# The last batch's shared result in an attention and mixture-of-experts kernel: four parts behind the last expert, each with its own addition to the output

## The chip, the cores and the metric

The kernel runs on one core of a Trainium2 chip. The metric is the device time of one execution in microseconds (us). Before the change three timed runs gave 1715.2, 1713.54 and 1716.4, a median of 1715.2. The profile is of one further execution.

## The reference

Input x has 4 batches of 512 tokens with 512 features; a context of 4 x 1601 rows goes with it. The layer is a cross attention (16 heads; an image part and a text part of the context with a softmax each) added to x, and then a mixture of experts added to the result:

```python
x = x + _L0_xattn_ref(_layernorm(x), ctx_2048, ...)
x = x + _L0_ffn_ref(_layernorm(x), ...)
```

The second part matters here. A router picks 4 of 32 experts for each of the 2048 tokens, each expert takes at most 80 tokens, and a shared expert runs over all tokens:

```python
G = jnp.einsum('ecd,edi->eci', Xp, W_gate)
U = jnp.einsum('ecd,edi->eci', Xp, W_up)
Y = jnp.einsum('eci,eid->ecd', jax.nn.silu(G) * U, W_down)
Yf = Y.reshape(EC, d) * slots_w[:, None]
out = jnp.zeros((T, d), x.dtype).at[slots_token].add(Yf)
shared = jax.nn.silu(x @ shared_gate.T) * (x @ shared_up.T) @ shared_down.T
return (out + shared).reshape(b, s, d)
```

Everything is in float32. The output is 2048 rows of 512 numbers, 2 KB a row.

## The kernel before

The attention of the four batches comes first and takes most of the time. The program writes the order of work of every engine out by hand: small functions are called one after another, and each engine (TensorE for matmuls, ScalarE, VectorE, GpSimd and SyncE, which issues most DMAs) runs its instructions in that order, waiting for others by semaphores.

The mixture of experts takes some 380 us at the end. First come the shared expert's parts for the first three batches (`units`), with the routing of the tokens between them. `shared` (L923) makes for each batch four `gate` parts (L945), four `up` parts (L954) and four `down` parts (L965), each one a product of four matmuls into one PSUM bank. `gate` applies Silu on ScalarE into a tile hT, `up` multiplies by the second product on VectorE. For batches 0 to 2 (`n < BEFORE`) `down` adds the stored attention result and writes 128 rows of the output with a plain DMA from SyncE's queue (L976). For batch 3 the attention result is already in the output (L457), and `down` copies its product by ScalarE into a tile `ys` (L980). The fourth `down` of that batch issues one DMA on GpSimd's queue that adds all 512 rows, 1 MB, to the output in memory (L983). In that tile a partition holds four consecutive rows of the output, 8 KB; to bring this about, `gate` and `up` of batch 3 read their PSUM bank in steps of four tokens (`by_token` and `as_tiles`, L934 and L937).

`shared` returns two lists. The first, `units`, runs in a loop at L1071. The second, `between`, holds the twelve parts of batch 3, and runs inside the loop over the experts at L1099. One turn of that loop does, for expert e: `gate_up(e)` (16 matmuls over 80 tokens), the issue of the gate and up weights for expert e + 5, on SyncE's queue (five buffers for each weight), `gather(e + 7)`, an indirect DMA on GpSimd's queue that fetches the tokens of a later expert, `turn(e + 2)`, which transposes gathered tokens, `down(e - 1)`, and then as many parts of `between` as are due by a count.

`down(e)` of an expert (L1029) scales its product on ScalarE into a tile `y` (four buffers) and issues an indirect DMA on GpSimd's queue that adds its 80 rows to the output (L1037). Each such addition may touch any row of the output, so each waits until the one before it has landed, whichever kind that was. The additions thus form a line on GpSimd's queue, with the gathers between them: additions of experts 0 to 25, the addition of `ys`, additions of experts 26 to 31.

The parts that are due are counted by

```python
while done < n_between and done * (E - 4) < n_between * e:
    between.pop(0)()
    done += 1
```

With 12 parts in `between` they come behind the experts' down parts at e = 1, 3, 5, 8, 10, 12, 15, 17, 19, 22, 24 and 26. PSUM's eight banks are handed out in turn (`psum`, L125), and the large tiles `wide` (L138) and the row tiles `rowt` (L147, five buffers) as well.

Of the kernel before, what the change touches and what calls it, by code (L numbers as in the profile page):

```python
# [12 lines left out]
AF = mybir.ActivationFunctionType  # L13
ALU = mybir.AluOpType
# [4 lines left out]
P = 128  # L19
B, L, D = 4, 512, 512  # L20
# [6 lines left out]
NQ = L // P  # L27
# [31 lines left out]
@with_exitstack  # L59
def xattn_moe_kernel(ctx: ExitStack, tc: tile.TileContext, a: dict, out: bass.AP):  # L60
    nc = tc.nc

    dram = ctx.enter_context(tc.tile_pool(name="dram", bufs=1, space=DRAM))
    x1_d = dram.tile([T, D], F32, name="x1_d")

    xw_d = dram.tile([T, D + E], F32, name="xw_d")
    xnT_d = dram.tile([P, NC, T], F32, name="xnT_d")
    den_d = dram.tile([B * NC, 2 * NG4, L], F32, name="den_d")
    rec_d = dram.tile([B * NC, 2 * NG4, L], F32, name="rec_d")

    const = ctx.enter_context(tc.tile_pool(name="const", bufs=1))
    ident = const.tile([P, P], F32, name="ident")
    make_identity(nc, ident)
    mhalf = const.tile([P, 8], F32, name="mhalf")
    nc.gpsimd.memset(mhalf, -0.5)
    logits = const.tile([P, NT, E], F32, name="logits")

    with tc.manual_schedule():
        body(tc, a, ident, mhalf, logits, x1_d, xw_d, xnT_d, den_d, rec_d, out)


BEFORE = 3
# [27 lines left out]
def body(ctx, tc, a, ident, mhalf, logits, x1_d, xw_d, xnT_d, den_d, rec_d, out):  # L110

    nc = tc.nc
# [12 lines left out]
    def psum(dt=F32):  # L125

        shape = [P, 512] if dt is F32 else [P, NQ, P]
        banks.append(banks.pop(0))
        return ring.tile(shape, dt, name="ps", tag=f"bank{banks[-1]}")
# [8 lines left out]
    def wide(name, keep=False):  # L138

        n = wides.pop(0)  # L140
        t = pt.tile([P, NC, 512], F32, name=name, tag=f"wide{n}")
        if keep:
            return t, n
        wides.append(n)
        return t
# [4 lines left out]
    def held(name):  # L150
        return hold.tile([P, D], F32, name=name, tag="hold")
# [9 lines left out]
    def weight(name, tile_=None, tag=None):  # L161
        t = w.tile([P, NC, D], F32, name=name, tag=tag or name) if tile_ is None else tile_
        nc.sync.dma_start(t, a[name])
        return t
# [14 lines left out]
    _, n, s0, _ = BLOCKS[0]  # L179
# [42 lines left out]
    def project(ps, lhsT, rhs):  # L222

        for c in range(NC):
            nc.tensor.matmul(ps, lhsT=lhsT(c), rhs=rhs(c), start=c == 0, stop=c == NC - 1)
# [447 lines left out]
    for n in range(2):  # L673
        t = w.tile([P, NQ, P], BF16, name=f"parts{n}", tag=f"parts{n}")
# [6 lines left out]
    for b in range(B):  # L681
# [88 lines left out]
        for bl in range(NB):  # L770
            for c in range(NC):
# [7 lines left out]
                n = 7 if bl < 2 else 0  # L779
# [143 lines left out]
    def shared():  # L923


        units = [[], []]
        downs = []
        xTs = {0: first_xT[0]}

        def fetch_x(n):  # L930
            xTs[n] = wide("xT")
            nc.sync.dma_start(xTs[n], xnT_d[:, :, n * L:(n + 1) * L])

        def by_token(hT, ic):  # L934
            return hT[:, ic, :].rearrange("p (j q) -> p j q", q=P)

        def as_tiles(ps, n):  # L937


            return ps.rearrange("p (j q) -> p j q", q=P) if n < BEFORE else ps.rearrange("p (q j) -> p j q", j=NQ)  # L940

        for n in range(B):
            t = {}

            def gate(ic, n=n, t=t):  # L945
                if ic == 0:
                    t["hT"] = wide("hT")
                if ic == 2 and n + 1 < B:
                    fetch_x(n + 1)
                ps = psum()  # L950
                project(ps, lambda k: sg[:, k, ic * P:(ic + 1) * P], lambda k: xTs[n][:, k, :])
                nc.scalar.activation(by_token(t["hT"], ic), as_tiles(ps, n), AF.Silu)

            def up(ic, n=n, t=t):  # L954
                ps = psum()
                project(ps, lambda k: su[:, k, ic * P:(ic + 1) * P], lambda k: xTs[n][:, k, :])
                nc.vector.tensor_tensor(by_token(t["hT"], ic), by_token(t["hT"], ic), as_tiles(ps, n), ALU.mult)
                if n == 0 and ic == NC - 1:
                    wides.append(first_xT[1])

            def fetch(j, n=n, t=t):
                t[j] = held("x1r")
                nc.sync.dma_start(t[j], x1_d[n * L + j * P:n * L + (j + 1) * P, :])

            def down(j, n=n, t=t, fetch=fetch):  # L965
                rows = slice(n * L + j * P, n * L + (j + 1) * P)
                if n < BEFORE:
                    if j == 0:
                        fetch(0)
                    if j + 1 < NQ:  # L970
                        fetch(j + 1)
                ps = psum()
                project(ps, lambda k: t["hT"][:, k, j * P:(j + 1) * P], lambda k: sd[:, k, :])
                if n < BEFORE:
                    nc.vector.tensor_tensor(t[j], t[j], ps, ALU.add)
                    nc.sync.dma_start(out[rows, :], t[j])  # L976
                    return
                if j == 0:
                    t["ys"] = wide("ys")
                nc.scalar.copy(t["ys"][:, j, :], ps)  # L980
                if j == NQ - 1:
                    to = out[n * L:(n + 1) * L, :].rearrange("(p j) d -> p j d", j=NQ)
                    nc.gpsimd.dma_start(to, t["ys"], accum_op=ALU.add)  # L983

            to = units[n >= BEFORE]
            if n == BEFORE:
                units[0] += downs
                downs = []
            for ic in range(NC):
                to += [partial(gate, ic), partial(up, ic)]  # L990
                if ic < 2:
                    to += downs[2 * ic:2 * ic + 2]
            downs = [partial(down, j) for j in range(NQ)]
        units[1] += downs
        return units

    def expert_parts():
# [48 lines left out]

        return weights, gather, turn, gate_up, down

    units, between = shared()
    wo = weight("o_w", wide("wo"))  # L1050
    for u in units[:2]:
        u()
# [46 lines left out]
    for e in range(E + 1):  # L1099
# [12 lines left out]
        while done < n_between and done * (E - 4) < n_between * e:  # L1112
            between.pop(0)()
            done += 1

# [1 line left out]


# [33 lines left out]
```

## Time and profile before

| what | us |
|---|---|
| median of three timed runs | 1715.2 |
| time of the profiled execution | 1718.64 |
| its span | 1716.8 |
| TensorE busy in it | 1681.6 (98%) |
| GpSimd busy | 864.1 (50%) |
| VectorE busy | 981.4 (57%) |
| ScalarE busy | 650.6 (38%) |
| first addition of an expert's result issued at | 1491.44 |
| addition of the last batch's shared result issued at | 1675.39 |
| last addition of an expert's result issued at | 1709.25 |

Times inside the profile count from the start of the span. A line in order of time gives start, duration, engine, source line, operation, the names written and read, the count, and in brackets how long the engine had been idle and what ended that. PE is TensorE, PEld its weight load, ACT is ScalarE, DVE VectorE, POOL GpSimd, SP SyncE. A busy TensorE is one that has matmuls in its pipeline, not one at its peak. In a table of stretches each row gives the window, then the busy time of the five engines with their numbers of instructions, the clock granted to TensorE, the mean share of time that the 16 DMA engines were busy, and GB/s. A line of a DMA queue gives packets, MB and the time that these packets took as a share of the 16 engines' window.

### The profile page before, as it was taken

The page shows a single profiled execution, that of the slowest core. Times are in us where ns is not written, and L with a number is a line of the kernel's source. Part 1 is how long each engine was busy: PE and PEld are TensorE (multiplying, and loading weights), DVE is VectorE, ACT ScalarE, POOL GpSimd, SP SyncE. Part 2 cuts the span into 40 slices and gives each one's busy share as a digit, 9 for nine tenths or more (in the row PEclk, how much of TensorE's full clock was granted, in tenths as well). Part 3 has the DMA queues.
Part 4 walks back from the last instruction along what each step waited for, and adds up shares of the span by engine and source line. Part 5 has one row for each costly group of instructions (what it writes and reads, how often), then busy time and mean ns, then how long its engine had stood idle before and what let it go on. Part 6 is the DMA issues. An engine that isn't in the chain of part 4 may idle for free. (4 is left out here: it accounts for less than half of the span.)

```text
span 1716.8 us, 29451 instructions
## 1 busy us (share of the span) xinstructions
PE 1681.6 (98%) x11753; PEld 881.2 (51%) x11753; DVE 981.4 (57%) x2016; ACT 650.6 (38%) x1378; POOL 864.1 (50%) x615
## 2 busy tenths in 40 slices
PE   8999999999999999999999999999999999999995
PEld 4554444456544444565444445644443454677774
DVE  3765554857555557976665579676657667111100
ACT  2135456611454565114555651145547210011111
POOL 3246977333669853337688533286793110233322
PEclk9999999999999999999999999999999999999998
DMA  7000000312000004020000040300002463599883
GB/s 232 1 1 1 27 27 2 114 64 70 30 2 26 26 3 163 19 77 20 5 24 27 15 152 21 105 14 15 2 14 89 145 230 132 176 271 278 264 258 61
DMA packets 67961, 137.35 MB, mean 80 GB/s; under 512 B 16112, under 2 KB 28528, under 8 KB 65648
## 3 DMA queue, kind: packets, MB, share of 16 engines
q1 hardware_dynamic: 61552, 122.01, 21.2%
q0 software_dynamic: 5264, 11.87, 3.6%
q8 instruction: 93, 1.52, 0.4%
q10 hardware_dynamic: 1008, 1.59, 0.3%
q14 instruction: 44, 0.36, 0.1%
HBM read 112.63 MB, written 22.81 MB: 79 GB/s over the span
## 5 line engine op out<-in xcount | busy, mean ns | idle before, releaser
L372 ACT ACTIVATE pT<-ps 128x512 f32<-128x512 f32 (+1 forms) x832 | 429.5, 604 | 342.5 <-PE ps L371 332.0
L334 DVE TENSOR_REDUCE mx<-ps 128x1 f32<-128x512 f32 (+1 forms) x576 | 330.9, 616 | 265.0 <-PE ps L320 265.0
L387 POOL TENSOR_TENSOR acc<-acc,pT 128x1024 f32<-128x1024 f32 x192 | 445.6, 2359 | 3.0 <-ACT pT L372 2.6
L379 PE MATMUL po<-pT,v 128*32 128x512 f32 (+2 forms) x1792 | 222.0, 603 | 0.0
L290 PEld LDWEIGHTS ps<-v_w,cT 128*128 128x128 f32 (+1 forms) x1408 | 168.9, 186 | 102.2 <-DVE mx L334 56.1
L371 PE MATMUL ps<-qT,kT 32*128 32x512 f32 (+1 forms) x1664 | 213.8, 587 | 0.0
L320 PE MATMUL ps<-kT,qT 32*128 32x512 f32 (+1 forms) x1536 | 206.1, 549 | 0.0
L290 PE MATMUL ps<-v_w,cT 128*128 128x128 f32 (+1 forms) x1408 | 197.7, 284 | 0.0
L231 PE MATMUL ps<-cT,wk 128*128 128x512 f32 (+1 forms) x384 | 156.9, 554 | 6.0 <-DMA wk<-in_k_w 6.0
L308 DVE TENSOR_REDUCE mx<-ps 128x1 f32<-128x512 f32 (+2 forms) x256 | 128.1, 562 | 5.2 <-PE ps L305 5.2
L1037 POOL DMA_INDIRECT out<-y,tok x32 | 45.5, 1422 | 149.2 <-DMA out<-y,tok 84.0
L231 PEld LDWEIGHTS ps<-cT,wk 128*128 128x128 f32 x384 | 70.6, 193 | 76.4 <-issue 55.3
L1027 DVE TENSOR_TENSOR ehT<-ehT,ps 128x160 f32<-128x160 f32 x32 | 10.3, 321 | 172.9 <-ACT ehT L1026 134.4
L368 PEld LDWEIGHTS <-pick 32*128 32x128 bf16 (+1 forms) x832 | 21.6, 91 | 165.7 <-issue 164.0
L298 ACT COPY v<-ps 128x128 f32<-128x128 f32 (+1 forms) x208 | 60.1, 289 | 117.7 <-PE ps L290 117.3
L238 POOL TENSOR_TENSOR sq_k<-sq_k,sq 128x512 f32<-128x512 f32 (+2 forms) x48 | 49.6, 1033 | 103.7 <-ACT sq L235 103.4
L394 POOL TENSOR_TENSOR acc<-pT 128x1024 f32<-128x1024 f32 x24 | 56.1, 2360 | 86.9 <-ACT pT L372 54.3
L387 POOL TENSOR_TENSOR pT<-pT 65x1024 f32<-65x1024 f32 x24 | 56.0, 2350 | 86.8 <-PE po L379 78.0
L387 DVE TENSOR_TENSOR acc<-acc,pT 128x1024 f32<-128x1024 f32 (+1 forms) x72 | 97.7, 1404 | 2.1 <-ACT pT L372 2.1
L320 PEld LDWEIGHTS ps<-kT,qT 32*128 32x128 f32 x1536 | 82.0, 183 | 30.8 <-issue 10.1
L379 PEld LDWEIGHTS po<-pT,v 128*32 128x32 f32 (+2 forms) x1792 | 34.7, 107 | 118.6 <-issue 109.3
L368 PE MATMUL ps<-mT,pick 32*128 32x512 bf16 (+1 forms) x832 | 82.5, 385 | 2.4 <-ACT mT L359 2.4
(209 smaller groups left out, 2188.8 us busy)
## 6 DMA issues: line engine op xcount, KB each, us to landing
W_gate<-in_W_gate SPq DMA_DIRECT2D x32, 512.0 KB
W_up<-in_W_up SPq DMA_DIRECT2D x32, 512.0 KB
W_down<-in_W_down SPq DMA_DIRECT2D x32, 512.0 KB
rb<-rec_d SPq DMA_DIRECT2D x64, 128.0 KB
xt<-in_x SPq DMA_DIRECT2D x30, 256.0 KB
cT<-in_ctxT SPq DMA_DIRECT2D x7, 1024.0 KB
wki<-in_k_img_w SPq DMA_DIRECT2D x4, 1024.0 KB
wo<-in_o_w SPq DMA_DIRECT2D x4, 1024.0 KB
```

The lines of the kernel that those rows point to most:

```text
L231: nc.tensor.matmul(ps[:, :n], lhsT=wt[:, k, c * P:(c + 1) * P], rhs=xT[:, k, to], start=k == 0, stop=k == NC - 1)
L290: nc.tensor.matmul(ps[lo:hi, :], lhsT=cTs[bl][:, k, at:at + hi - lo], rhs=ws[bl == NB - 1][:, k, c * P:(c + 1) * P], start=k == 0, stop=k ...
L298: nc.scalar.copy(v[:n, t, :], ps[:n])
L308: nc.vector.tensor_reduce(mx[:, qt, g, bl:bl + 1], ps[:, :n], AX.X, ALU.max, negate=True)
L320: nc.tensor.matmul(ps[:, j * n:(j + 1) * n], lhsT=qT[r:r + HD, c, q * P:(q + 1) * P], rhs=kT[r:r + HD, c, k0:k0 + n], start=True, stop=True,)
L334: nc.vector.tensor_reduce(mx[:, qt, g, i:i + 1], ps[:, :m], AX.X, ALU.max, negate=True)
L368: nc.tensor.matmul(ps[:n], lhsT=pick[r:r + HD, kind(t), :n], rhs=mT[r:r + HD, :], start=True, stop=False)
L371: nc.tensor.matmul(ps[:n], lhsT=kT[r:r + HD, c, t * P:t * P + n], rhs=qT[r:r + HD, c, :], start=False, stop=True)
L372: nc.scalar.activation(pT[:n, g, :], ps[:n], AF.Exp)
L379: nc.tensor.matmul(po[r:r + HD, :], lhsT=v[rows, t, r:r + HD], rhs=pT[rows, g, :], start=start, stop=stop)
L387: (nc.vector if idle else nc.gpsimd).tensor_tensor(to[rows, h, :], to[rows, h, :], pT[rows, h, :], ALU.add)
L394: (nc.vector if idle else nc.gpsimd).tensor_tensor(acc[:, h, :], pTs[0][:, h, :], pTs[1][:, h, :], ALU.add)
```

## The change

The four `down` parts of batch 3 leave the list that runs inside the expert loop. They form a third list, `ends`, which runs after the loop, behind the last expert. Each of them copies its product into a row tile of its own and issues an addition of its own, on GpSimd's queue, to its 128 rows of the output (256 KB, 2 KB a row). `gate` and `up` read PSUM and write hT in plain order for every batch. With 8 parts left in `between`, the count puts them behind e = 1, 4, 8, 11, 15, 18, 22 and 25. Of the four new additions the first waits for the last expert's addition and for its copy, the others for their copies alone.

```diff
-        units = [[], []]
+        units = [[], [], []]
...
-                nc.scalar.activation(by_token(t["hT"], ic), as_tiles(ps, n), AF.Silu)
+                nc.scalar.activation(t["hT"][:, ic, :], ps, AF.Silu)
...
-                nc.vector.tensor_tensor(by_token(t["hT"], ic), by_token(t["hT"], ic), as_tiles(ps, n), ALU.mult)
+                nc.vector.tensor_tensor(t["hT"][:, ic, :], t["hT"][:, ic, :], ps, ALU.mult)
...
-                if j == 0:
-                    t["ys"] = wide("ys")
-                nc.scalar.copy(t["ys"][:, j, :], ps)
-                if j == NQ - 1:
-                    to = out[n * L:(n + 1) * L, :].rearrange("(p j) d -> p j d", j=NQ)
-                    nc.gpsimd.dma_start(to, t["ys"], accum_op=ALU.add)
+                y = rowt("ys")
+                nc.scalar.copy(y, ps)
+                nc.gpsimd.dma_start(out[rows, :], y, accum_op=ALU.add)
...
-            to = units[n >= BEFORE]
-            if n == BEFORE:
+            to = units[n == B - 1]
+            if n == B - 1:
...
             downs = [partial(down, j) for j in range(NQ)]
-        units[1] += downs
+            if n >= BEFORE:
+                units[2] += downs
+                downs = []
...
-    units, between = shared()
+    units, between, ends = shared()
...
+    for f in ends:
+        f()
```

More of the change, by code (lines that the diff above doesn't have):

```diff
@@ L932, in fetch_x @@
             nc.sync.dma_start(xTs[n], xnT_d[:, :, n * L:(n + 1) * L])
[L934 to L940, printed above, removed]
         for n in range(B):
```

## Prediction

> **What bounds the kernel now.** I read the page first, then the chain of waits, then the last 240 us by stretches and in order of time. The profiled execution has a span of 1716.8 us and a time of 1718.64; the three timed runs have a median of 1715.2. I make the sum on the span and carry the difference over to 1715.2. What a measurement of this kernel can tell from no change is about 0.2%, 3.4 us.
>
> The chain that ended last, and the stretches around the experts:
>
> ```profile
> DMA out<-y,tok 1%; POOLq L1148 0%; POOLq L1037 0%
> ```
>
> ```profile
> core 0: us, PE busy (x) PEld busy (x) DVE busy (x) ACT busy (x) POOL busy (x), PEclk, DMA share, GB/s
> 1500.00:1660.00 160.00, 160.00 (x994) 116.56 (x993) 19.34 (x50) 25.66 (x52) 53.02 (x45) 1.00 0.90 272
> 1661.00:1671.20 10.20, 10.20 (x61) 7.21 (x61) 0.72 (x2) 2.23 (x4) 1.89 (x2) 1.00 0.86 276
> 1671.20:1675.40 4.20, 4.20 (x30) 3.12 (x30) 0.72 (x2) 0.30 (x1) 0.93 (x2) 1.00 0.35 43
> 1690.47:1709.25 18.78, 8.19 (x43) 4.92 (x41) 0.52 (x2) 2.35 (x4) 5.64 (x4) 0.80 0.28 35
> ```
>
> The chain sees only the end: expert results added to the output (L1037), each held by the one before. The stretches show why TensorE is not the end. It is occupied until some 1698, while the DMA engines, 0.90 busy with weights until 1671, drop to 0.28 in the last 19 us, where nothing but those additions is left. The same additions in order of time, on GpSimd's queue:
>
> ```profile
> 1627.43 1.42 POOL L1037 DMA_INDIRECT out<-y,tok  x1 [5.09 <-ACT y L1036]
> 1629.16 0.93 POOL L1002 DMA_INDIRECT xp<-xw_d,tok  x1 [0.30 <-issue]
> 1635.64 1.42 POOL L1037 DMA_INDIRECT out<-y,tok  x1 [5.56 <-DMA out<-y,tok]
> 1642.92 1.42 POOL L1037 DMA_INDIRECT out<-y,tok  x1 [4.63 <-DMA out<-y,tok]
> ...
> 1670.73 1.39 POOL L1037 DMA_INDIRECT out<-y,tok  x1 [5.51 <-ACT ys L980]
> 1675.39 0.95 POOL L983 DMA_DIRECT2D out<-ys  x1 [3.27 <-issue]
> 1685.80 1.47 POOL L1037 DMA_INDIRECT out<-y,tok  x1 [9.45 <-DMA out<-ys]
> 1690.47 1.42 POOL L1037 DMA_INDIRECT out<-y,tok  x1 [3.20 <-ACT ehT L1026]
> ...
> 1709.25 1.41 POOL L1037 DMA_INDIRECT out<-y,tok  x1 [3.32 <-DMA out<-y,tok]
> ```
>
> The column to read is the start. Quiet, one addition follows another after 1690.47 - 1685.80 = 4.67; from 1685.80 to 1709.25 there are five such steps, 4.69 each. With weights in flight it is 8.21 (1627.43 to 1635.64) or 7.28. Additions 1 (issued at 1500.40) to 25 (1670.73) take 170.33 us, 7.10 a step. The single addition of the last batch's shared result, 1 MB, holds the queue from 1675.39 to 1685.80: 10.41. So the line of additions ends the kernel, and from addition 2 (1507.20) on its 1716.8 is: 23 steps (163.53) + 4.66 + 10.41 + five quiet steps (23.45) + 7.55 from the last issue to the end.
>
> TensorE sets when each y exists:
>
> ```profile
> 1666.26 3.60 PE L225 MATMUL ps<-shared_down,hT 128*128 128x512 f32 x8
> ...
> 1669.69 1.91 PE L225 MATMUL ps<-xpT,W_gate 128*128 128x80 f32 x16
> ...
> 1675.22 1.91 PE L225 MATMUL ps<-xpT,W_gate 128*128 128x80 f32 x16
> ...
> 1680.75 1.91 PE L225 MATMUL ps<-xpT,W_gate 128*128 128x80 f32 x16
> ```
>
> An expert costs it 1680.75 - 1675.22 = 5.53, a shared part 1669.69 - 1666.26 = 3.43.
>
> **The change, part by part.** *Down parts to the end.* Four parts of 3.43 leave the expert loop and follow the last expert; TensorE's sum is unchanged and still ends near 1698.7, with the last copy to ys (0.59 on ScalarE) by 1699.9. In place of twelve parts the loop holds eight, behind experts 1, 4, 8, 11, 15, 18, 22, 25 instead of 1, 3, 5, 8, 10, 12, 15, 17, 19, 22, 24, 26. The first part stands where it stood, so nothing moves before addition 2 at 1507.20. Behind it TensorE runs at 5.53 + 8 x 3.43 / 25 = 6.6 an expert instead of 7.10, and asks for weights that much faster.
>
> *The addition to the end.* The 10.41 between additions 25 and 26 goes; the queue runs on from 25 to 26 in an ordinary step. It comes back behind addition 31: the first of the four waits for addition 31 to land and for its ys; the other three wait only for ScalarE's copies, so they are issued together, as nine gathers in the trace were, 1.21 us apart. The bytes are the same 1 MB, in rows of 2 KB instead of 8. Bounds: the four quiet steps from 1690.47 to 1709.25 keep the engines busy 0.28 x 18.78 / 4 = 1.31 us for the 164 KB of one, 3.38 of a step being waits around it; 1 MB in such rows is 8.4 us, and 11.8 with the waits. From below, the old addition itself in the window 1676.30 to 1685.80:
>
> ```profile
> q0 software_dynamic: 144, 1.05, 59.8%
> ```
>
> 59.8% of 9.50 us is 5.7 for 1.05 MB on GpSimd's queue, 9.1 with the waits; the rest went to a weight load beside it. I take the row of the same bytes, 10.41, between them. From its landing to the end there are 7.55 - 4.69 = 2.86 as now. So this move alone costs nothing: 10.41 leaves the middle and 10.41 returns.
>
> *What is left: the steps.* Between 1507.20 and the end the new kernel has 29 steps up to addition 31, then 4.69 for its landing, 10.41 and 2.86. It equals the old one when the 29 steps take 1716.8 - 1507.2 - 17.96 = 191.64 us. Steps under weights cost p each, quiet ones 4.69. The weights of the last expert's gate and up are gone at 1671.2 (share 0.86, then 0.35); three fewer parts stand ahead of them, 10.3 us, so quiet could begin at 1661. With L = length under weights (153.8 to 1661) the 29 steps take L + (29 - L/p) x 4.69; they equal 191.64 at p = 7.34.
>
> *The price p.* Of the 24 steps from addition 1 to 25, eighteen ended with the landing of the addition before; they average 7.17 (6.62 to 8.21). The other six ended only when y came: there the line had caught up with TensorE. In the new kernel TensorE runs ahead and the line never catches up, so every step is of the first kind. And weights are denser: 0.90 x 7.10 / 6.6 = 0.97 of the DMA engines. The excess over quiet, 2.48, grows as this does, to 2.67, p = 7.36. Then the stretches without a shared part: two or three experts long now, three or four afterwards. The steps that begin behind the first expert of today's stretches of three are 7.54, 7.00, 7.07, 7.95, 8.21 and 7.28, mean 7.51, or 7.73 with the excess scaled alike. With 14 experts in the first two places of a stretch at 7.36 and 10 in later places at 7.73, p = 7.51. Stretches of four lie beyond what the trace shows, and its longest step is 8.21; I take 7.6. At 0.97 the weights themselves come late by some 2 us, so quiet begins at 1663, L = 155.8.
>
> Sum: 155.8 + (29 - 20.5) x 4.69 = 195.7, against 191.64: **+4.0**. Span 1720.8, time 1715.2 + 4.0 = 1719.2.
>
> *Costed at nothing.* Silu and product of the last batch write hT straight (ScalarE 0.60 in all 16 runs of L952 and VectorE 0.66 to 0.69 in those of L957, old order and plain alike). The four copies to ys lie on ScalarE while the line is at additions 26 to 31; uncovered they would cost 0.59 each. y has four buffers: with the line some 20 us behind, ScalarE's y 27 waits a few us for addition 23, and what is queued behind it is the next expert's Silu; TensorE has 20 us of idle tail before that touches the end. SP issues the same loads in the same order; gathers stay ahead by seven experts.
>
> The Trainium skill ("DMA: Bandwidth & Descriptors", Anatomy of one DMA) puts a fixed cost of about 2.0 us and bytes / 436e3 on each transfer issued by GpSimd, and asks for 1 MiB at a time. By it one transfer is 4.4 and four in line 10.4, an estimate of +6.0 for this change. This trace has the single one at 10.41, beside weights, so above the page's figure.
>
> **The rivals.** *The line gains (faster).* Place: the steps from 1507 to 1661. In the stretches with the engines full (share 0.98 to 1.01) the steps are 7.00, 7.18, 6.68 and 6.69, mean 6.89: a full queue need not mean long steps. Then 153.8 + (29 - 22.3) x 4.69 = 185.2, -6.4, time 1708.8. It decides from p below 7.34. Against it: these windows contain a shared part each. TensorE sets the floor: a last ys at 1699.9 and a quiet addition, 4.69 + 2.86 + 0.8 for its extra rows, end at 1708.3, -8.5.
>
> *It evens out.* p stays at 7.17 and quiet begins at 1661: 189.2, -2.4, time 1712.8. For it: the interference is that of a fixed number of weight bytes. Against it: six cheap steps are lost.
>
> *The four additions go in line.* If each is held until the one before has landed, each costs 4.69 + 0.8 = 5.5, 22.0 for 10.41: +11.6 on top of -2.4, time 1724.4. For it: one queue, one tensor. Against it: their rows are disjoint and no wait is written. (The page's fixed cost would work this way.)
>
> **How the numbers follow.** Forecast (p above 7.5) 0.40, gains 0.23, evens out 0.30, in line 0.07. Faster by over 0.2%: 0.23. Within: 0.30. Slower: 0.47. The range runs from 1708, just beyond the gaining line, to 1726: p = 8.0 with quiet at 1663 is 155.8 + (29 - 19.5) x 4.69 = 200.4, +8.7, and 1.4 more for a tail at its upper bound, 1725.3; the additions in line lie inside. The forecast's own range, 1717 to 1726, starts where the tail is at its lower bound and p at 7.55.
>
> **What would show it.** Right: addition 23 issued near 1663, steps under weights near 7.6, quiet steps 4.7, addition 31 near 1703, four issues of ys 1.2 apart near 1707, TensorE idle from 1699. Wrong: steps under weights of 7.3 or less, additions again released by ScalarE, ys waiting for ys, or TensorE stopped by late weights before 1661, which would lengthen everything.

## The result and the profile after

| | before | changed |
|---|---|---|
| median of 20 timed runs, us | 1716.6 | 1709.35 |
| lowest and highest | 1712.83, 1720.87 | 1708.25, 1717.04 |
| span of the profiled execution | 1716.8 | 1706.7 |

The ratio is 0.9968, with a 95% interval of 0.9958 to 0.9978: faster by 0.3%, where +0.2% was forecast. Measured again later (experiment 8), the changed kernel gave 0.9975 (0.9965 to 0.9986). Of the 20 runs of the changed kernel in the table, thirteen lie at 1708 to 1710 and seven at 1713 to 1717; the profile is of one of the thirteen, and no trace shows what the seven do differently. The spans differ by 10.1 us and the medians by 7.3, because the profile before is of an execution 2.0 us above its median (1718.64) and the one after 1.0 below (1708.38). What follows is read from the profiles.

The page of the changed kernel still ends with the line of additions:

```profile
DMA out<-y,tok 1%; POOL out L972 0%; POOLq L1140 0%; POOLq L1028 0%; POOLq L972 0%
```

The line itself, on GpSimd's queue in order of time (start, duration, engine, line, operation, in brackets the idle time before):

```profile
1506.95 1.41 POOL L1028 DMA_INDIRECT out<-y,tok  x1 [4.73 <-issue]
...
1583.84 1.42 POOL L1028 DMA_INDIRECT out<-y,tok  x1 [4.79 <-DMA out<-y,tok]
...
1588.44 1.42 POOL L1028 DMA_INDIRECT out<-y,tok  x1 [1.95 <-ACT ehT L1017]
...
1621.50 1.42 POOL L1028 DMA_INDIRECT out<-y,tok  x1 [4.82 <-DMA out<-y,tok]
...
1629.66 1.42 POOL L1028 DMA_INDIRECT out<-y,tok  x1 [5.51 <-DMA out<-y,tok]
...
1650.58 1.42 POOL L1028 DMA_INDIRECT out<-y,tok  x1 [5.85 <-DMA out<-y,tok]
...
1662.05 1.39 POOL L1028 DMA_INDIRECT out<-y,tok  x1 [3.58 <-ACT y L1027]
...
1690.09 1.39 POOL L1028 DMA_INDIRECT out<-y,tok  x1 [3.15 <-DMA out<-y,tok]
1694.53 2.74 POOL L972 DMA_DIRECT2D out<-ys  x3 [3.05 <-DMA out<-y,tok]
1698.75 0.86 POOL L972 DMA_DIRECT2D out<-ys  x1 [1.48 <-ACT ys L971]
```

Addition 2 is issued at 1506.95 (1507.20 before), addition 23 at 1650.58 (1657.18), addition 25 at 1662.05 (1670.73), addition 31 at 1690.09 (1709.25). So 8.7 us are gained by addition 25: 6.4 in the 21 steps from addition 2 to 23 (143.63 us instead of 149.98) and 2.1 in the two steps behind them, where the weights end sooner. Between additions 25 and 31, where the 1 MB stood, 10.5 more are gained, and the end gives 9.1 back: 16.61 us follow addition 31 instead of 7.55. Steps under weights spread widely: 8.16 from 1621.50, but 4.60 from 1583.84, as cheap as a quiet one, in the midst of the weights. From addition 2 on every y is ready 2 to 10 us before its addition; an engine named in the brackets there had long been done.

Its stretches (window, busy time of the engines, clock, share of the DMA engines, GB/s):

```profile
1500.00:1660.00 160.00, 160.00 (x1042) 120.06 (x1042) 20.79 (x54) 25.81 (x52) 54.00 (x46) 1.00 0.92 288
1660.00:1670.00 10.00, 10.00 (x79) 8.49 (x78) 0.72 (x2) 1.79 (x4) 2.78 (x2) 1.00 0.44 93
1670.00:1680.00 10.00, 10.00 (x70) 7.84 (x69) 1.04 (x3) 1.86 (x4) 2.78 (x2) 1.00 0.28 35
```

288 GB/s instead of 272, and the DMA engines are quiet from the 1660s. TensorE (1042 matmuls in the first window instead of 994) never stops for weights there.

### The profile page after: what moved, and what is told of

The parts are those of the page before. It is cut to its first block, busy times and chain, and to the rows that moved or that the text cites. A ratio compares the mean times of both kernels' runs of the same rounds, so it can differ in the third digit from the quotient of the medians.

```text
span 1706.7 us, 29452 instructions
## 1 busy us (share of the span) xinstructions
PE 1681.3 (99%) x11753; PEld 881.2 (52%) x11753; DVE 981.0 (57%) x2016; ACT 651.1 (38%) x1378; POOL 866.9 (51%) x618
## 5 line engine op out<-in xcount | busy, mean ns | idle before, releaser
L1018 DVE TENSOR_TENSOR ehT<-ehT,ps 128x160 f32<-128x160 f32 x32 | 10.3, 321 | 158.5 <-ACT ehT L1017 158.5
L394 POOL TENSOR_TENSOR acc<-pT 128x1024 f32<-128x1024 f32 x24 | 56.1, 2360 | 86.9 <-ACT pT L372 54.3
L320 PEld LDWEIGHTS ps<-kT,qT 32*128 32x128 f32 x1536 | 82.0, 183 | 30.8 <-issue 10.1
## 6 DMA issues: line engine op xcount, KB each, us to landing
wki<-in_k_img_w SPq DMA_DIRECT2D x4, 1024.0 KB, 10.5
```

The lines of the kernel that those rows point to most:

```text
L320: nc.tensor.matmul(ps[:, j * n:(j + 1) * n], lhsT=qT[r:r + HD, c, q * P:(q + 1) * P], rhs=kT[r:r + HD, c, k0:k0 + n], start=True, stop=True,)
L394: (nc.vector if idle else nc.gpsimd).tensor_tensor(acc[:, h, :], pTs[0][:, h, :], pTs[1][:, h, :], ALU.add)
```

## The experiments

The theories are A: the line was held up by y, and TensorE running ahead is what helped. B: the 1 MB addition in the middle of the line was what cost. D: dense weights set the length of the steps, as the prediction had it. C, F, G and H are stated where they are tested. Ratios are to the kernel before, with 95% intervals.

### 1. The additions moved alone

```diff
-                nc.gpsimd.dma_start(out[rows, :], y, accum_op=ALU.add)
+                units[2].append(lambda: nc.gpsimd.dma_start(out[rows, :], y, accum_op=ALU.add))
...
-                units[2] += downs
+                units[1] += downs
```

> The four down parts stay inside the expert loop at their old places (TensorE 7.10 us an expert); only the four additions go behind the last expert's. Theory A (the line of additions lost some 11 us waiting for y, and TensorE running ahead is what removed that): the steps up to addition 25 stay as before, addition 25 near 1670.7, the y of experts 26 to 31 come every 5.53, so addition 31 near 1702.7 and the span near 1719, a ratio of 1.000 to 1.002. Theory B (the 1 MB addition in the middle of the line was what cost): the span falls to 1706 to 1709 as in the changed kernel, a ratio near 0.996.

Ratio 1.0016 (1.0007 to 1.0025), span 1719.4. The end of its line:

```profile
1676.88 1.39 POOL L1028 DMA_INDIRECT out<-y,tok  x1 [6.48 <-ACT y L1027]
1682.41 1.39 POOL L1028 DMA_INDIRECT out<-y,tok  x1 [4.14 <-ACT y L1027]
...
1707.15 3.62 POOL L972 DMA_DIRECT2D out<-ys  x4 [2.71 <-DMA out<-y,tok]
```

Freed of the 1 MB, the line waits for y, 5.53 us an expert from 1676.88 on, and the four additions then come on top. B falls: moving the additions without the parts loses 0.2%.

### 2. The parts last, with one addition

```diff
-        units[1] += downs
+        units[2] += downs
...
+    for f in ends:
+        f()
```

> The four down parts go behind the last expert, but their result is added in one addition of 1 MB with rows of 8 KB, as before the change. Theory A: steps up to addition 31 as in the changed kernel (1690 for addition 31); the one addition waits for the last copy (1698.5) instead of starting at 1694.5, so the span is 4 to 6 us above the changed kernel's, near 1712, a ratio of 0.997. Theory C (the small rows and four issues cost more than they save): the span is at or below the changed kernel's 1706.7, a ratio of 0.995 or less.

Ratio 0.9971 (0.9959 to 0.9983), span 1709.8. Addition 31 is issued at 1690.17, as in the changed kernel, and the one addition when the last copy is done:

```profile
1698.54 0.96 POOL L983 DMA_DIRECT2D out<-ys  x1 [6.98 <-ACT ys L980]
```

It ends 11.3 us later; the changed kernel has three of its four under way by then, for a span 3.1 us shorter in the profiles (4 to 6 expected). The intervals of the two ratios overlap, so what this part of the change is worth isn't clear of the noise. C, that small rows cost more than they save, asked for a span of 1706.7 or less and a ratio of 0.995 or less, and falls by both.

### 3. TensorE ahead, the addition in the middle

Left out are the four down products; hT is copied to ys, and the 1 MB is added behind expert 25.

```diff
-                ps = psum()
-                project(ps, lambda k: t["hT"][:, k, j * P:(j + 1) * P], lambda k: sd[:, k, :])
...
-                nc.scalar.copy(t["ys"][:, j, :], ps)
+                nc.scalar.copy(t["ys"][:, j, :], t["hT"][:, j, :])
...
-        units[1] += downs
+        units[2] += downs
...
+        if e == 26:
+            for f in ends:
+                f()
```

> Left out: the down products of the last batch (hT is copied to ys instead). gate and up stand at the changed kernel's places, so TensorE runs ahead as there, but the 1 MB addition stays behind expert 25. Theory A: the steps to addition 25 are as in the changed kernel (near 1662), then 5 + 10.4 + 5 x 4.65 + 7.55, span near 1708, a ratio of 0.995. Theory B: the line still has the 1 MB in its middle, so the span stays near 1716, a ratio of 1.000.

Ratio 0.9948 (0.9934 to 0.9962), span 1707.0:

```profile
1663.17 1.39 POOL L1037 DMA_INDIRECT out<-y,tok  x1 [3.15 <-DMA out<-y,tok]
1667.67 0.95 POOL L983 DMA_DIRECT2D out<-ys  x1 [3.11 <-issue]
1676.01 1.47 POOL L1037 DMA_INDIRECT out<-y,tok  x1 [7.39 <-DMA out<-ys]
```

Addition 25 is about where A put it (1662 expected). With the addition where it always was, the kernel (which has four products fewer to make) is as fast as the changed one: what helps is TensorE's lead, which gives 7.6 of the 9.8 us by addition 25. The 1 MB takes 1676.01 - 1667.67 = 8.34 here, with no weight load beside it, instead of 10.41.

### 4. The first part behind expert 4

```diff
-        while done < n_between and done * (E - 4) < n_between * e:
+        while done < n_between and done * (E - 7) < n_between * (e - 3):
```

> The changed kernel with the eight parts of the loop behind experts 4, 7, 10, 13, 16, 19, 22, 25 instead of 1, 4, 8, ...: the one wait for y that is left, before addition 1 (the addition before it had landed some 3.4 us earlier), goes. Theory A (the end follows the line, and every wait for y in it is worth its length): addition 1 near 1496.1 instead of 1499.55, span 3.4 us below the changed kernel's, near 1703.3, a ratio of 0.992 to 0.994 to before. Theory D (the weights that are in flight set the pace of the line, whatever it waits for): the saved time is lost again in longer steps, span 1706 to 1708, a ratio near 0.996.

Ratio 0.9961 (0.9947 to 0.9974), span 1708.2: no gain over the changed kernel. The wait before addition 1 is gone, but the step there is 8.02 instead of 8.97, since addition 0 now meets weights (the last of its rows is through 6.5 us after the issue instead of 4.3), and addition 31 is at 1691.43. These are D's numbers, though its reason is not the only one: the last of the four additions is held by ScalarE's last copy.

```profile
1699.54 0.86 POOL L972 DMA_DIRECT2D out<-ys  x1 [1.07 <-ACT ys L971]
```

### 5. All twelve parts last

```diff
+    ends = between + ends
+    between = []
```

> The changed kernel with all twelve parts of the last batch (gate, up and down) behind the last expert. TensorE then asks for an expert's weights every 5.53 us, more than the DMA engines give (0.92 busy at 6.6 us an expert), so weights come late and TensorE's end moves from 1698 to 1702 to 1704. Theory A (the line has no wait for y left to lose; the end is TensorE's end and 8 us): span 1709 to 1713, ratio near 0.997. Theory D (denser weights lengthen the line's steps to 7.6 and more, as the prediction had it): steps under weights 7.6 to 8.2, addition 31 behind 1700, span 1715 or more.

Ratio 1.0008 (0.9999 to 1.0018), span 1719.6. Both theories missed; D's span came by another path. Two of its stretches, a line of its waits (who waited for whom: us in total, times, longest), and its last additions:

```profile
1520.00:1540.00 20.00, 20.00 (x143) 15.68 (x143) 2.88 (x8) 3.29 (x8) 7.71 (x7) 1.00 1.04 340
...
1600.00:1620.00 20.00, 18.54 (x120) 14.11 (x120) 1.51 (x5) 2.10 (x5) 6.20 (x6) 0.92 0.91 292
```

```profile
ACT y L1027 <- DMA out<-y,tok: 86.9, 18, 7.1
```

```profile
1701.81 0.95 POOL L972 DMA_DIRECT2D out<-ys  x1 [12.58 <-ACT ys L971]
...
1712.15 0.86 POOL L972 DMA_DIRECT2D out<-ys  x1 [2.62 <-ACT ys L971]
```

From addition 2 (1505.48) to 20 (1633.37) the line steps 7.10 on average, neither 7.6 to 8.2 nor 6.8, and not one of the eighteen steps is under 6. The thirteen up to 1599.16, with the DMA engines full (a share of 1.02 as the profile counts it), average 7.21; the five behind them, at 0.91, 6.84. TensorE runs so far ahead that y's four buffers are taken: ScalarE waits 86.9 us for additions to land, TensorE stops with it from 1580 on, and its end moves to 1711. The line is done at 1692 and the kernel waits for TensorE.

### 6. Before the change, without the 1 MB

Left out is the addition of the last batch's shared result.

```diff
-                    nc.gpsimd.dma_start(to, t["ys"], accum_op=ALU.add)
+                    pass
```

> The kernel before the change with its 1 MB addition left out (the last batch's shared result never reaches the output; all products and copies stay). Theory A: behind addition 25 the line is soon waiting for y, which comes every 5.53 us (the last at 1699.4), so of the 10.4 us only some 6 to 7 are saved: addition 31 near 1702.7, span near 1710, ratio 0.996. Theory B (the 10.41 us are the whole of it): span near 1706.4, ratio 0.994.

Ratio 0.9965 (0.9953 to 0.9978), span 1708.8, 8.0 below before: between A's 7 and B's 10.4. Additions 26 to 30 wait for y, as A has it; but TensorE and y came 1.2 us earlier in this execution from addition 0 (1490.27) on. By the distance from addition 0, the end is 6.8 us nearer, and the medians differ by 6.0; both are A's.

### 7. The changed kernel without weight loads

Left out are the loads for experts 5 to 31.

```diff
+            if e >= WEIGHTS:
...
+                weights.setdefault(e, []).append(weights[e - WEIGHTS][i])
+                continue
```

> The changed kernel with the weights of experts 5 to 31 not loaded (each takes those of the expert five before). The line then runs quiet and follows TensorE; the first of the four additions could start at 1690 instead of 1694.5. Theory F (in the changed kernel TensorE's end, 1698.5 for the last copy, and one addition behind it have become the floor): the span stays within 1.5 us of the changed kernel's, 1705.5 to 1707. Theory G (the line still sets the end): the span falls by the 4.8 us that the line gains, to 1702.

Ratio 0.9952 (0.9935 to 0.9968), span 1706.1: F. The line now follows y and is done 2.3 us earlier (1692.21 instead of 1694.53); the last addition still starts when TensorE lets it.

```profile
1692.21 1.86 POOL L976 DMA_DIRECT2D out<-ys  x2 [3.07 <-DMA out<-y,tok]
...
1698.58 0.86 POOL L976 DMA_DIRECT2D out<-ys  x1 [2.62 <-ACT ys L975]
```

### 8. The changed kernel again

> The changed kernel itself, on the same chip as the three above: span near 1707, ratio 0.996 to 0.997, the line behind y from addition 2 on with steps under weights of 6.7 to 7.0 on average, some of them 4.6 to 5.8.

Ratio 0.9975 (0.9965 to 0.9986), span 1707.9, median of ten runs 1713.04. From addition 2 (1506.28) to 23 (1650.33) the steps average 6.86, four of them under 5.4; one addition, number 4 (1520.03), still waited for y.

### 9. Before the change, with the line two steps late

The additions of experts 0 and 1 are issued twice, so their rows count double.

```diff
-            nc.gpsimd.indirect_dma_start(
...
+            for _ in range(2 if e < 2 else 1):
+                nc.gpsimd.indirect_dma_start(
...
```

> The kernel before the change with the additions of experts 0 and 1 issued twice each (so those rows count double in the output). This puts two more steps, 13 to 14 us, at the head of the line and changes nothing for TensorE, which stays at 7.10 us an expert. Theory A (a step of the line without any wait for y is 6.7 to 6.9 us on average, short ones of 4.6 to 6 among them; the 7.17 were an average over the late steps alone): the line wins most of it back by addition 25, which is issued 2 to 4 us later than before (near 1673), and the span rises by 2 to 4 us, to 1719 to 1721, ratio 1.001 to 1.003. Theory D (a late line pays 7.2 to 7.6 for every step, as the prediction had it): addition 25 near 1678 to 1684, span up by 7 to 13 us, ratio 1.004 to 1.008.

Ratio 1.0019 (1.0007 to 1.0031), span 1720.7. Expert 2's addition is at 1516.78, expert 25's here:

```profile
1676.91 1.39 POOL L1038 DMA_INDIRECT out<-y,tok  x1 [3.27 <-DMA out<-y,tok]
1681.37 0.95 POOL L983 DMA_DIRECT2D out<-ys  x1 [3.07 <-ACT y L1036]
1689.83 1.47 POOL L1038 DMA_INDIRECT out<-y,tok  x1 [7.51 <-ACT ehT L1026]
```

The span is A's, the path is not. Never waiting, the line steps 7.03 from expert 2 to 23 (147.6 over 21 steps), against 7.14 with its waits (149.98): of the 9.6 us by which it is late at expert 2, it wins 3.4 back by expert 25 (1676.91 against 1670.73). The rest comes from the 1 MB, 8.46 in place of 10.41. So the waits for y explain a part of the gain only; three of the 21 steps are under 6.

### 10. The changed kernel without the down products

Left out are the four products behind the last expert; hT is copied to ys.

```diff
-                ps = psum()
-                project(ps, lambda k: t["hT"][:, k, j * P:(j + 1) * P], lambda k: sd[:, k, :])
...
-                nc.scalar.copy(y, ps)
+                nc.scalar.copy(y, t["hT"][:, j, :])
```

> Left out: the four down products behind the last expert (hT is copied to ys instead; the four additions stay). TensorE ends 13.7 us earlier, near 1685, and all four additions go out together when addition 31 has landed, near 1694.5. Theory F2 (line and TensorE are level in the changed kernel, the line a little ahead): span 0 to 1.5 us below the changed kernel's 1706.7. Theory G (TensorE's end alone holds the changed kernel, with the line several us to spare): span 1703 or less. Theory H (the line alone holds it): no change at all, 1706.7 to 1707.

Ratio 0.9967 (0.9954 to 0.9979), span 1706.4. All four go out at once, and the end is where it was:

```profile
1693.80 3.63 POOL L972 DMA_DIRECT2D out<-ys  x4 [2.86 <-DMA out<-y,tok]
```

G is out. The span alone doesn't tell F2 from H, but in 7 the freed line brought nothing either, which leaves F2: in the profiled executions of the changed kernel line and TensorE are level, and taking the work from either leaves the span within 0.6 us. The timed medians on the chip of these runs say less: 1713.04 for the changed kernel (8), 1711.3 here, 1707.74 without weight loads (7, four runs). By them freeing the line gains some 5 us, so the balance is shown for the profiled executions alone.

## Why the prediction was wrong

**What held.** The line ended the kernel before; in the changed one it ends level with TensorE's last copy. The move of the addition alone is no gain (experiment 1: 0.2% slower; forecast at nothing). Addition 2 stayed within 0.3 us of its place. Three of the four additions go out with no wait between them (2.74 us for three), so the rival of additions in line is out. Quiet steps stayed at 4.5 to 4.7. Quiet began at some 1660, about when the parts moved by 10.3 us let it (1661); the 2 us that the prediction put on top for late weights had no row behind them.

**The step that failed: the price p of a step under weights.** The prediction took 7.6, and the changed kernel has 6.84 (1506.95 to 1650.58, 21 steps), on the side of 7.3 that the prediction had named as its sign of being wrong; five more profiles with TensorE ahead (experiments 2, 3, 4, 8 and 10) have 6.84, 6.91, 6.75, 6.86 and 6.84. The 29 steps up to addition 31 came to 183.1 us instead of 195.7, and that is 12.6 of the 14.1 us by which the span was missed. Put p = 6.84 and quiet at 1661 into the prediction's own formula and it gives 153.8 + (29 - 22.5) x 4.69 = 184.3.

Three things went into 7.6, and none of them stood. Of the 0.76 us a step that it was too long, the two surcharges on 7.17 make 0.43 and the choice of the late steps alone 0.14 (experiment 9: 7.03); the other 0.19 stay open.

*"Every step is of the first kind."* The 7.17 was an average over the eighteen steps that ended with a landing. In the other six, y came after the landing, and those were cheap steps with a wait behind them: in the trace before, the additions ahead of these six had their last rows through 3.5 to 4.7 us after the issue, quiet ones 3.5 to 3.6, those ahead of the other eighteen 5.3 to 6.8. A step seen from its end only counts as late if it was long; the average is over the long ones. In the changed kernel the line never catches up, and yet five of the 21 steps are between 4.60 and 5.76; the other sixteen average 7.34, close to the 7.36 that the prediction gave to the first two places of a stretch.

*Stretches of four without a part.* The longest step was 8.50, but the stretches of four didn't raise the average: from addition 3 to 7, 10 to 14 and 17 to 21 it is 6.72, and experiment 4, with stretches of three alone, has 6.75.

*Denser weights.* The engines were 0.93 busy from addition 2 to 23, where 0.97 had been forecast. At 1.02, with the pauses gone too (experiment 5), the average was 7.21 instead of 6.84: a small effect, far from 8.

**Where the short steps come from.** The one looked at most closely meets a pause in the weights. SyncE's queue, which issues each weight load when TensorE has used the old one, in the changed kernel around the step of 4.60:

```profile
1580.74 0.33 SPq L908 DMA_DIRECT2D W_down<-in_W_down  x1
1585.92 0.33 SPq L908 DMA_DIRECT2D W_gate<-in_W_gate  x1
```

Between these two TensorE does a shared part (3.43 us) and asks for nothing. The stretches show that step, the part of it in which the addition's rows move, and the step from 1621.50:

```profile
1583.84:1588.44 4.60, 4.60 (x39) 4.11 (x38) 0.39 (x2) 0.90 (x2) 2.35 (x2) 1.00 0.71 170
1585.83:1587.28 1.45, 1.45 (x15) 1.45 (x15) 0.00 (x0) 0.00 (x0) 0.67 (x1) 1.00 0.92 119
1621.50:1629.66 8.16, 8.16 (x43) 5.17 (x42) 0.72 (x2) 1.01 (x3) 2.34 (x2) 1.00 1.00 345
```

The short step moves 170 GB/s in all, and 119 while the addition's rows move, against 345 in the long one. The five short steps of the changed kernel end with additions 7, 10, 14, 17 and 21, one for each of the parts behind experts 8, 11, 15, 18 and 22. Without parts in the loop no step under weights is under 6 (experiment 5, where the engines are fuller as well). A step with less traffic need not be short: 7.90 at a share of 0.79 in experiment 9 (from 1566.21), so it seems to matter when in the step the pause falls. With twelve parts and a line that never waits there are three such steps and 7.03 on average (9), with eight parts five and 6.84. Why fewer pauses caught more additions, by the distance that the line keeps behind y it seems, was not tried and stays open.

**The tail.** Forecast: 17.96 from addition 31 to the end; measured 16.61. The 1 MB was priced by a row that had a weight load beside it: 10.41, while alone it takes 8.34 and 8.46 (3 and 9). Some of that went to a wait for ScalarE's last copy, 1698.47, which the prediction put at 1699.9 and let lie hidden, since its line came late enough. It is the floor that the rival of the gaining line named: the end is 8.2 us behind that copy. The rival itself took p = 6.89 from the stretches with full engines and said 1708.8; the median is 1709.35. That it came so near is luck in part: full engines don't make steps short (7.21 in experiment 5), and the short steps that were found lie in pauses.

The Trainium skill ("DMA: Bandwidth & Descriptors", Anatomy of one DMA) would have four transfers of 256 KB cost an estimated 6.0 us more than one of 1 MB, if they went in line. Here one takes 11.26 from its issue to the end (experiment 2, 1698.54 to 1709.8), four together 12.6 (experiment 10, 1693.80 to 1706.4): 1.3 us more. So they did not go in line, and the measurement decides.

## What to carry to other kernels

A line of transfers that each wait for the last is slowed by its producer, by other traffic and by what is put in its middle; let the producer run ahead and the other traffic end sooner before moving pieces of the line itself. Don't price a step by the cases in which it was seen to be late: delay the line on purpose and measure every step. When two chains end level, as line and TensorE do in these profiles, taking work from one brings nothing more.

## What was not expected

With the DMA engines full (a share of 1.02 in experiment 5) the additions stepped 7.21 us, hardly more than the late steps at 0.90 in the kernel before (7.17). And loading no weights at all (experiment 7) shortened the profiled span by 0.6 us only, though the median by 5.3 (against experiment 8).
